# Zero-weight products of a hybrid layer kernel left out from the fifth chunk to the end of the scans

## The chip, the cores and the metric

The kernel runs on one core of a Trainium2 chip. The metric is the device time of one execution in microseconds (us). The core has five engines with a queue each: TensorE (PE, matrix products; its weight loads are listed as PEld), VectorE (DVE), ScalarE (ACT), GpSimd (POOL) and SyncE (SP, which here only issues transfers). Transfers (DMA) are issued from SP and POOL.

## The reference, cut to what matters

The input is x with 8 images of 256 channels and 1024 tokens. Layer 0 is a Mamba block with a forward layer; layer 1 is attention with eight heads and a routed pair of experts for each image.

```python
# layer 0, each image
xz = layernorm(x) @ W_in;  xm, z = split(xz)             # 512 + 512 channels
xm = silu(causal_conv4(xm) + conv_b)
dt, Bm, Cm = split(xm @ W_x);  dt = softplus(dt @ W_dt + b_dt)
for t in tokens:                                          # 16 states a channel
    h = exp(dt[t] * A) * h + (dt[t] * xm[t]) * Bm[t]
    y[t] = sum_s(h * Cm[t])
x = ((y + xm * D) * silu(z)) @ W_out + x
x = gelu(layernorm(x) @ W1 + b1) @ W2 + b2 + x
# layer 1
t = x + attention(ln(x), column bias from edges)          # 8 heads of 32, 1024 x 1024 scores
t = t + layernorm(experts(ln(t)) + ln(t))                 # top 2 of 8, chosen per image
```

## The kernel before

All values are float32 and lie with the channels on the 128 partitions. Tokens are worked in chunks of 512, two to an image, 16 in all (`i` from 0 to 15). In the program a product of float32 operands is one instruction; the profile shows it as two passes (841 zero products in the program, 1682 passes).

**The backbone.** The loop `for now in range(nsteps)` goes over 512 scan steps, 32 to a chunk (`NSTEP`): a step is one of 16 states and one of two halves of the 512 channels. VectorE multiplies the inputs with a row of B (`hb<-xm,bc`), scans over the 512 tokens with the decay from ScalarE (`da_all<-dt,vecs`), and multiplies with the row of C (`hb<-hb,bc`). An accumulating transfer on POOL's queue adds the result up in memory (`dx<-hb`). `bc` is a row of B and of C, broadcast to all partitions by a transfer on SP's queue two states ahead.

**The streams beside it.** All other work is written as generators: `prologue` (norm `mu_a`, `var_a`, projection `xin`, convolution, `dbl`, `v`, softplus), `gate_part` (`z`, silu), `epilogue` (output `mo`, norm `mu_f`, `var_f`, forward layer `fh`, `facc`, norm `mu_t`, `var_t`), attention (`vp`, `qkp`, scores `sc`, exponentials `pt`, sums `num` and `den`, output `wo`, norm `mu_x`, `var_x`) and experts (`he`, `re`, norm `var_y`). In each norm VectorE subtracts a mean that TensorE has just formed (`tn_t<-fo,mu_t` for instance), and works on the variance after it.

**What sets the order.** A planner at build time (`Model`, `Queue`) keeps a clock for each engine with a cost for each kind of instruction, steps its time along VectorE's queue in `advance`, and writes the next piece of a stream when the planned time has come and its buffers and banks are free. Each engine then runs its instructions in the order written. There are two single banks of PSUM (`banks`), two pairs (`pairs`) for scores, and one bank each for `num` and `den`.

**Zero products.** At the end of each planner tick `advance` calls `keep_warm` (L1794). Where TensorE's planned time lies more than 0.2 us behind, it writes one product of 128 x 128 zero weights with 256 columns of a constant. While an attention sum is open it adds zeros to that bank (`num<-mean_c,zero_c` in the profile), else it takes a free single bank and gives it back at once (`warm<-mean_c,zero_c`).

```python
if pe.at > model.t - 0.2:
    return
x = mean_c.to_broadcast([P, CH // 2])
if open_sums:
    pe.matmul(open_sums[-1][:, : CH // 2], zero_w, x, start=False, stop=False)
elif banks.ready():
    ps = banks.now("warm")
    pe.matmul(ps[:, : CH // 2], zero_w, x, start=True, stop=True)
    model.end = pe.at
    banks.put(ps)
```

After the scans `while due: idle(0.25)` (L1947) lets the streams that are left run out: the last image's attention and experts, where the sums of exponentials are on VectorE. A second way to compute (`attention_any` and the block after it) is taken only when a flag on the data asks for it, and does not run here.

Of the kernel before, what the change touches and what calls it, by code (L numbers as in the profile page):

```python
# [28 lines left out]
NSTEP = NHALF * NS  # L29
# [25 lines left out]
def hybrid_kernel(ctx: ExitStack, tc: tile.TileContext, a: dict, out: bass.AP):  # L55
# [21 lines left out]
    model = Model()  # L77
# [40 lines left out]
    pool, pe = Queue(nc.gpsimd, pool_cost), Queue(nc.tensor, pe_cost)  # L118
# [351 lines left out]
            vec.tensor_scalar(w[:, k, cols], w[:, k, cols], V(gain, k), None, ALU.mult)  # L470

    capacity = float(math.ceil(B * L * 1.25 / E))
    set_up = []
    open_sums = []
    ends = {}
# [260 lines left out]
    def load_bc(n):  # L736
        i, s = divmod(n, NS)
        bc = work_pool.tile([P, 2, CH], F32, name=f"bc_{n}", tag="bc", bufs=AHEAD + 1)
        landed = sp.dma_start(
            bc, chunk[i]["bc_d"][s].partition_broadcast(P)  # L740
        )
        bcs[n] = (bc, landed)
# [6 lines left out]
    def decay(g, q):  # L749
        i, s, h = place(g)  # L750
        da = da_all[:, g % 2, q, :]
        n = (2 * h + q) * NS + s


        skip = 1 if q and i % NCH == 0 else 0
        if skip and g % NSTEP < 2:
            act.copy(da[:, :1], zero_c)
        act.activation(
            da[:, skip:], chunk[i]["dt"][h][:, q, skip:], AF.Exp, scale=neg_a[:, n : n + 1]
        )  # L760
        das[g, q] = act.at
        if q and s == NS - 1:
            model.end = act.at
            t4.put(chunk[i]["dt"][h])

    def inputs(g):

        i, s, h = place(g)
        hb = hbs[g] = h4.now(f"hb_{g}")
        bc, landed = bcs[g // NHALF]  # L770
        vec.at = max(vec.at, landed)
        xd = chunk[i]["xd"][h]
        vec.tensor_tensor(hb, xd, bc[:, 0, :].unsqueeze(1).to_broadcast([P, 2, CH]), ALU.mult)
        if s == NS - 1:
            t4.put(xd)

    def scan(g, q):

        i, s, h = place(g)
        c = i % NCH  # L780
        hb = hbs[g]
        d = 2 * h + q
        done = das.pop((g, q))
        vec.at = max(vec.at, done)
        if c == 0:
            if q:
                both = hb.rearrange("p a t -> p (a t)")
                vec.tensor_tensor_scan(
                    both, da_all[:, g % 2].rearrange("p a t -> p (a t)"), both, 0.0,
                    ALU.mult, ALU.add,  # L790
                )
        else:
            vec.tensor_tensor_scan(
                hb[:, q, :], da_all[:, g % 2, q, :], hb[:, q, :], state[:, s, d : d + 1],
                ALU.mult, ALU.add,
            )
        if q and c < NCH - 1:
            pool.tensor_copy(state[:, s, 2 * h : 2 * h + 2], hb[:, :, CH - 1])

    def sums(g):  # L800

        i, s, h = place(g)
        me = chunk[i]
        bc, _ = bcs[g // NHALF] if h < NHALF - 1 else bcs.pop(g // NHALF)
        hb = hbs.pop(g)
        vec.tensor_tensor(hb, hb, bc[:, 1, :].unsqueeze(1).to_broadcast([P, 2, CH]), ALU.mult)
        model.t = vec.at
        me["landed", h] = pool.dma_start(out=me["acc", h], in_=hb, accum_op=ALU.add)
        h4.put(hb, at=me["landed", h])

    def gate_part(i):

        while not set_up:
            yield POLL
        me = chunk[i]
        mem = Owner(t4, 3, 2)
        xn = yield from mem.take(f"xz_{i}")
        yield sp.dma_start(xn, me["xn_d"])
        sz, ps = [], None
        for d in range(ND + 1):  # L820
            if d:
                h, q = divmod(d - 1, 2)
                act.activation(
                    sz[h][:, q, :], ps, AF.Identity, bias=b_in[:, ND + d - 1 : ND + d]
                )
                banks.put(ps)
            if d < ND:
                if d % 2 == 0:
                    sz.append((yield from mem.take(f"sz_{i}_{d // 2}")))
                ps = yield from banks.take(f"z_{i}_{d}")  # L830
                for k in range(KC):
                    pe.matmul(
                        ps, w_in[:, k, DI + d * P : DI + (d + 1) * P], xn[:, k, :],
                        start=(k == 0), stop=(k == KC - 1),
                    )
                yield
        mem.put(xn)
        for t in sz:
            act.activation(t, t, AF.Silu)
        lnexp()  # L840
        mem.end()
        yield
        me["sz"] = sz
# [916 lines left out]
    with tc.tile_pool(name="work", bufs=1) as work_pool:  # L1760
# [30 lines left out]
        def start(stream, key, at=0.0):  # L1791
            due.append([at, URGENT[key[0]], len(done) + len(due), stream, key])

        def keep_warm():  # L1794


            if pe.at > model.t - 0.2:
                return
            x = mean_c.to_broadcast([P, CH // 2])
            if open_sums:  # L1800
# [7 lines that stand above are left out]
        def advance():  # L1808


            while True:
                model.t = min(model.t + TICK, vec.at)
                for d in sorted(due, key=lambda d: d[1:3]):
                    while d in due and d[0] <= model.t + 0.05:
                        if d[1] > 2 and max(pe.at, act.at) > model.t + LAG:
                            break
                        model.end = model.t
                        try:
                            at = next(d[3])
                        except StopIteration:  # L1820
                            due.remove(d)
                            done.add(d[4])
                            break
                        if at == POLL:
                            break
                        d[0] = (model.end if at is None else at) + 0.1
                keep_warm()
                if model.t >= vec.at:
                    break

        def idle(t):

            vec.at += t
            advance()
# [77 lines left out]
        inputs(0)  # L1912
        for now in range(nsteps):
            i, k = divmod(now, NSTEP)
            if i + 1 < B * NCH and k == max(FRONT[i], 1):
                start(prologue(i + 1), ("p", i + 1), model.t)
            if k == GATE[i]:
                start(gate_part(i), ("g", i), model.t)
            n = now // NHALF + AHEAD
            if now % NHALF == 0 and n < B * NCH * NS:  # L1920
                while "bc_d" not in chunk.get(n // NS, {}):
                    idle(0.5)
                load_bc(n)
            if now + 2 < nsteps:
                while "dt" not in chunk.get((now + 2) // NSTEP, {}):
                    idle(0.5)
            for q in range(2):
                scan(now, q)
                advance()
                if now + 2 < nsteps and (q or i % NCH):  # L1930
                    for r in range(0 if i % NCH == 0 else q, q + 1):
                        decay(now + 2, r)
            if now == 0:
                while ("p", 0) not in done:
                    idle(0.25)
                for q in range(2):
                    decay(1, q)
            if now + 1 < nsteps:
                while not h4.free:
                    idle(0.5)  # L1940
                inputs(now + 1)
                advance()
            sums(now)
            if k == NSTEP - 1:
                start(epilogue(i), ("e", i), model.t)
            advance()
        while due:  # L1947
            idle(0.25)

# [264 lines left out]
```

## Time and profile before

| | us |
|---|---|
| median of 3 runs | 3561.6 |
| lowest and highest | 3555.06, 3567.71 |
| profiled execution, its own time | 3553.65 |
| its span, first to last instruction | 3551.9 |
| PE, DVE, ACT, POOL busy in it | 3227.3, 3062.4, 2470.0, 935.7 |
| mean granted TensorE clock | 0.953 |

The span is what views of the trace divide up; the execution's own time lies 1.75 us above it. Busy times of one engine don't overlap, those of several do. A wait is an idle stretch of an engine with what ended it. In the view by windows, each line has the stretch, its length, the busy time of each engine with the number of instructions, the granted clock (1 is full speed), the share of the DMA engines and GB/s. A product's end is modelled, so TensorE's busy share is not its share of peak.

### The profile page before, as it was taken

What the parts mean: (1) busy time and instruction counts of PE and PEld (TensorE: products, weight loads), DVE (VectorE), ACT (ScalarE), POOL (GpSimd) and SP (SyncE); (2) the same over time, 40 slices, a digit from 0 to 9 for tenths busy, and PEclk for the clock granted to TensorE, in tenths of its full rate; (3) what the DMA queues carried; (4) which work ended last, traced back from release to release, by engine and by line L of the source; (5) the groups of instructions that cost most, each with busy time, mean ns of one, the idle gap of its engine ahead of it and who ended that gap; (6) DMA issues with size and microseconds to landing.
All of it is one profiled execution on the core that took longest, in us unless ns stands there. A gap on an engine that the chain in (4) does not pass through costs nothing. (4 is left out here: it accounts for less than half of the span.)

```text
span 3551.9 us, 40220 instructions
## 1 busy us (share of the span) xinstructions
PE 3227.3 (91%) x14535; PEld 1401.8 (39%) x14535; DVE 3062.4 (86%) x3148; ACT 2470.0 (70%) x3563; POOL 935.7 (26%) x1058
## 2 busy tenths in 40 slices
PE   8767879997999899999999999999999999999997
PEld 5544344333433344333443334333433334334344
DVE  6979999899999798999999899989999999943551
ACT  5553737795778776787778867886688776864644
POOL 0232223222332124322322233223432332211010
PEclk9888989999999998999999999999999999999999
DMA  4757978787788778898787987889888878942120
GB/s 121 196 128 159 201 172 195 166 195 180 186 203 202 168 177 190 207 196 196 183 202 182 203 187 188 188 194 210 199 200 186 197 180 192 207 107 70 37 76 15
DMA packets 189504, 607.80 MB, mean 171 GB/s; under 512 B 27056, under 2 KB 38000, under 8 KB 189296
## 3 DMA queue, kind: packets, MB, share of 16 engines
q0 software_dynamic: 103968, 366.54, 53.3%
q1 hardware_dynamic: 85328, 238.60, 20.8%
q8 instruction: 116, 1.90, 0.2%
q14 instruction: 92, 0.75, 0.1%
HBM read 238.58 MB, written 62.39 MB: 85 GB/s over the span
## 5 line engine op out<-in xcount | busy, mean ns | idle before, releaser
L100 ACT ACTIVATE da_all<-dt,vecs 128x512 f32<-128x512 f32 (+1 forms) x1024 | 700.9, 717 | 436.3 <-DVE hb L100 433.1
L95 POOL DMA_DIRECT2D dx<-hb x512 | 444.5, 871 | 1671.2 <-DVE hb L100 1331.3
L100 DVE TENSOR_TENSOR hb<-hb,bc 128x1024 f32<-128x1024 f32 x512 | 625.9, 1222 | 36.9 <-POOL state L100 26.9
L100 DVE TENSOR_TENSOR_SCAN hb<-da_all,state,hb 128x512 f32<-128x512 f32 x512 | 632.2, 1271 | 8.5 <-ACT da_all L100 8.4
L100 DVE TENSOR_TENSOR hb<-xm,bc 128x1024 f32<-128x1024 f32 x512 | 619.2, 1209 | 10.4 <-DMA dx<-hb 10.2
L100 DVE TENSOR_TENSOR_SCAN hb<-da_all,hb 128x1024 f32<-128x1024 f32 x256 | 584.7, 2284 | 2.8 <-ACT da_all L100 2.8
L100 ACT ACTIVATE pt<-sc 128x1024 f32<-128x1024 f32 x512 | 494.1, 1017 | 91.9 <-PE sc L100 81.1
L100 PE MATMUL warm<-mean_c,zero_c 128*128 128x256 f32 x1368 | 411.4, 430 | 35.4 <-ACT dt L100 9.3
L100 PEld LDWEIGHTS warm<-mean_c,zero_c 128*128 128x128 f32 x1368 | 260.0, 206 | 201.4 <-PE warm L100 82.5
L100 PE MATMUL sc<-qk,qk 32*128 32x512 f32 x2048 | 323.5, 644 | 10.9 <-ACT pt L100 10.4
L100 PE MATMUL num<-pt,v 128*32 128x512 f32 x2048 | 280.9, 620 | 43.9 <-DVE ot L100 43.9
L100 POOL COPY state<-hb 128x2 f32<-128x2 f32 x256 | 207.2, 809 | 366.5 <-DVE hb L100 351.3
L100 PE MATMUL den<-pt,ecb 128*32 128x512 f32 x1792 | 243.8, 615 | 0.0
L100 PE MATMUL facc<-fh,w 128*128 128x512 f32 x512 | 231.4, 598 | 3.9 <-DVE xf_x L100 1.8
L100 PE MATMUL fh<-x_f,w 128*128 128x512 f32 x480 | 230.2, 609 | 4.2 <-DVE x_f L100 1.7
L100 PE MATMUL he<-xe,g 128*128 128x512 f32 x448 | 218.5, 612 | 3.6 <-DVE x_f L100 1.8
L100 ACT ACT_TABLE_LOAD x169 | 216.8, 1283 | 3.6 <-PEq L2201 0.7
L100 PE MATMUL re<-he,g 128*128 128x512 f32 x472 | 213.8, 596 | 2.3 <-DVE xn L100 2.2
L100 PEld LDWEIGHTS sc<-qk,qk 32*128 32x128 f32 x2048 | 95.4, 184 | 183.4 <-issue 75.8
L100 PE MATMUL mo<-sz,w_out 128*128 128x512 f32 x256 | 126.4, 639 | 25.8 <-DVE sz L100 24.6
L100 PEld LDWEIGHTS facc<-fh,w 128*128 128x128 f32 x512 | 94.6, 190 | 131.1 <-issue 119.5
L100 PEld LDWEIGHTS fh<-x_f,w 128*128 128x128 f32 x480 | 87.9, 192 | 131.2 <-issue 109.6
(364 smaller groups left out, 4280.4 us busy)
## 6 DMA issues: line engine op xcount, KB each, us to landing
dx<-hb POOLq DMA_DIRECT2D x512, 512.0 KB, 6.5
bc<-bc_d SPq DMA_DIRECT2D x256, 512.0 KB, 4.5
dt<-e POOLq DMA_DIRECT2D x38, 512.0 KB, 8.6
dt<-u POOLq DMA_DIRECT2D x30, 512.0 KB, 9.0
xe<-xf_d SPq DMA_DIRECT2D x28, 512.0 KB, 6.5
xn<-in_x SPq DMA_DIRECT2D x16, 512.0 KB, 7.9
xn_d<-xn SPq DMA_DIRECT2D x16, 512.0 KB, 4.6
xz<-xn_d SPq DMA_DIRECT2D x16, 512.0 KB, 7.2
```

Source lines behind the costliest of these rows:

```text
L95: f(*args, **kw)
L100: return f(*args, **kw)
```

## The change

From the 129th scan step on (`now == 4 * NSTEP`, the first of the fifth chunk) `keep_warm` returns at once, and after the last scan step it works again as before. The list `busy` is the switch. Nothing else is edited; since the planner counts each zero product in TensorE's time and in a bank's, the place of other instructions can move.

```diff
     capacity = float(math.ceil(B * L * 1.25 / E))
+    busy = []
     set_up = []
...
         def keep_warm():
-            if pe.at > model.t - 0.2:
+            if pe.at > model.t - 0.2 or busy:
                 return
             x = mean_c.to_broadcast([P, CH // 2])
...
         for now in range(nsteps):
             i, k = divmod(now, NSTEP)
+            if now == 4 * NSTEP:
+                busy.append(True)
             if i + 1 < B * NCH and k == max(FRONT[i], 1):
                 start(prologue(i + 1), ("p", i + 1), model.t)
...
             advance()
+        busy.clear()
         while due:
             idle(0.25)
```

## The prediction

> **What bounds the kernel now.** I read the page's busy shares and slices first, then three stretches by windows, then what VectorE waits for, then single products in the timeline. One core runs everything, so span and clock need no comparison between cores. On the page, TensorE (PE) seems the fullest engine, VectorE (DVE) the next:
>
> ```profile
> PE 3227.3 (91%) x14535; PEld 1401.8 (39%) x14535; DVE 3062.4 (86%) x3148; ACT 2470.0 (70%) x3563; POOL 935.7 (26%) x1058
> ...
> PEclk9888989999999998999999999999999999999999
> ```
>
> The first 65 us are setup, the scan's chunks run from there to 3134 us, and the fifth chunk's first input product starts at 838 us (counted along VectorE's hb products, 32 to a chunk). So the change acts between 838 and 3134. The windows view gives per stretch the length, then PE, weight loads, DVE, ACT, POOL busy, the granted clock, DMA share and GB/s. The second fence is the same view for the instructions that read the zero column alone:
>
> ```profile
> 838.00:3134.00 2296.00, 2150.03 (x9396) 882.36 (x9392) 2160.68 (x2091) 1751.53 (x2493) 689.18 (x764) 0.97 0.84 193
> 3134.00:3552.00 418.00, 386.87 (x1842) 167.17 (x1838) 152.46 (x298) 212.70 (x268) 32.77 (x35) 0.98 0.19 53
> ```
>
> ```profile
> 838.00:3134.00 2296.00, 199.57 (x628) 113.77 (x628) 2.07 (x11) 0.00 (x0) 0.97 0.84 193
> ```
>
> DVE is busy 2160.7 of 2296 us, 94%. PE is busy 2150.0, but some 200 of that are products with zero weights, so its own work is at most 1950 us, 85%. VectorE sets the pace, and what can change is its 135 us of idle time. Its waits in this stretch (us, times, longest):
>
> ```profile
> DVE hb L100 <- POOL state L100: 19.7, 6, 4.7
> DVE tn_t L100 <- PE mu_t L100: 19.4, 7, 4.4
> DVE xm L100 <- ACT dx L100: 13.0, 1, 13.0
> DVE x_f L100 <- PE mu_f L100: 8.4, 6, 2.4
> DVE xf_x L100 <- PE mu_x L100: 8.2, 4, 3.9
> ```
>
> Those on TensorE, with the smaller rows (var_y 5.6, var_t 4.0, vp 3.1, four rows of 0.4 to 1.0), sum to 51.8 us. The change can take part of them away or add to them.
>
> What makes such a wait is seen in the timeline. The same four passes of a 512-column mean take 1.88 us at full clock (mu_x) and about 3 us or more after an idle stretch (mu_t, mu_f; start, length, instruction, idle before):
>
> ```profile
> 858.39 3.97 PE L100 MATMUL warm<-mean_c,zero_c 128*128 128x256 f32 x16
> 868.28 3.52 PE L100 MATMUL mu_f<-x,mean_c 128*128 128x512 f32 x4 [5.92 <-DMA x<-in_x]
> ```
>
> ```profile
> 2524.07 4.21 PE L100 MATMUL warm<-mean_c,zero_c 128*128 128x256 f32 x8 [0.72 <-DVE z L100]
> 2528.07 3.00 PE L100 MATMUL mu_t<-fo,mean_c 128*128 128x512 f32 x4
> ```
>
> ```profile
> 2376.78 1.88 PE L100 MATMUL mu_x<-xr,mean_c 128*128 128x512 f32 x4
> ```
>
> [...]its clock record for the 2296 us has 23 stretches at 0.5 and nothing else below 1.0, in multiples of 3.4 us, 149.8 us together, which is the windows' 0.97 (1 - 0.5 x 149.8 / 2296).[...]
>
> **The change part by part.**
>
> 1. *Products removed.* The built program drops from 841 zero products to 519: 322 fewer, in 110 runs of about three, 644 passes of 256 columns (the trace shows 628 of them after 838). Nothing else is taken out: DVE 5680, ACT 5598, POOL 1201 and SP 665 instructions stay, every DMA among them. The early chunks and the tail after the scans keep theirs. PE gets up to 199.6 us back, but mostly where it would be idle: gaps between real products sum to 328 us there against 146 us now.
>
> 2. *Clock lost.* I cut the stretch into 672 windows of 3.41 us, in phase with the clock record, and took TensorE's busy share of each from its matmul records. With the zero products 19 windows lie under 0.4, without them 65.[...] So there are 14 stretches more, each as long as now (149.8 / 23 = 6.5 us), 91 us at least; at most 76 windows more, 259 us[...]. What cold time costs DVE: its waits on products that ran in or right after a cold stretch are 4.4, 3.8, 3.7, 3.2, 2.4, 1.9, 1.8, 1.8 and 1.8 us, 24.9 us over 149.8, or 0.17 us per cold us. The rest is hidden, since expert, attention and forward products end in ScalarE evictions and ScalarE is 76% busy. So the loss is 15 to 43 us; I take 22, for some 130 us more of cold time.
>
> 3. *Waits ahead of real products removed.* In front, a run delays a real product by one 256-column product in flight at most (two passes, 3.97 / 8 = 0.50 us), over 110 runs 55 us of PE time, of which DVE sees only what ends in a mean, a variance or a v projection. TensorE's own waits before zero products (on readers of the bank) add 12.6 us in 14 cases. The gain for DVE cannot exceed its waits on PE outside cold stretches, 51.8 - 24.9 = 26.9 us, and may be nothing. I take 8.
>
> 4. *Order moved.* The planner counts zero products in TensorE's time and gives them a bank, so without them other work is placed a little differently: of 5680 DVE instructions 4358 keep their place. Against the scan steps of 6 us, the experts' work lies 4 to 6 steps earlier from chunk 4 on, the attention exponentials 1.1 steps, forward layer and prologue within half a step. At the end nothing is gained: 96 exponentials are left after the last scan before and after, and 54 evictions of he. Loads on SP's queue move by up to 13 places and accumulating transfers on POOL's by up to 23; bc keeps its two steps of lead. A single collision in this stretch costs DVE 4.7 (state) to 13.0 us (dx), so this can go either way: 0, with 10 us on each side.
>
> 5. *Tail.* From 3134 to 3552 DVE is the one that waits and PE is the chain; its zero products remain. Cost 0, within a few us that item 4 covers.[...]
>
> Sum: +22 - 8 + 0 = **+14 us**. The profiled execution took 3553.65 us by its own time (span 3551.9 and 1.75 around it), which makes 3567.7. That execution lies 8 us under the median of the shown runs, 3561.6, and I put the difference on the median: **3576 us**, slower by 0.4%.
>
> **The rivals.** A change over 0.3%, some 10.7 us, is about what a measurement of this kernel can tell from none.
>
> *Zero products were in the way (faster).* One mechanism: real products start earlier where TensorE is behind, between attention and the mean products, and the planner's earlier placing makes it lasting. For it: 110 runs, 12.6 us of bank waits, mu_t held behind eight passes. Against it: of the nine waits listed, only one has a run directly in front; the others have num and den products or nothing. With item 3 at its bound and item 2 at its low end: 15 - 27 = -12, with a lucky order -22: about 3545. It decides once more than half of the 51.8 us goes away.
>
> *TensorE is covered (no change).* DVE instructions stand in an order where a late product is met by work of 1.2 to 2.3 us (one product or scan in flight), and 1.7 us is what four cold passes lose. If this hides nearly every new stretch, the loss falls to 8 and the gain cancels it: 3562.
>
> *The removed products are not the ones that hold the clock.* At 858 sixteen of them ran off in 4 us and the clock still fell. Most gaps over 5 us already end cold. Then item 2 is near zero and the result is rival one or two.
>
> *A long slow stretch.* [...]the clock stays low through whole projections, and attention falls behind: the 43 us end, with the order against it: 3605 or more.
>
> **How the numbers follow.** Slower by over 0.3%: 0.45 (the +14 case and the long slow stretch). No change: 0.28. Faster: 0.27. The range is from the faster rival to the 43 us end with no gain, 3543 to 3606, leaving out one in ten on each side.
>
> **What would show it.** Clock in the fifth to sixteenth chunk: 0.94 rather than 0.97 (about 280 us cold), PE's busy share at 88 to 92%, the four passes of mu_t and mu_f more often at 3 to 3.5 us than at 1.88. DVE's waits on mu, var and vp products up from 51.8 to about 66 us. The last scan at about 3148 us; the tail near 418. I am wrong if the clock stays at 0.96 or above, or if it falls and those waits do not grow, or if the difference lies in waits on POOL, DMA or in the tail: then the order decided.

## The result, and the profile after

The changed kernel takes 3584.86 us (median of 4 runs, 3579.59 to 3590.17) against 3558.78 us for the kernel before (4 runs): ratio 1.007, 95% interval 1.0044 to 1.0095, 26 us slower. The profiled execution took 3590.17 us with a span of 3588.2. It is the slowest of the four, and the profiled one of the kernel before, 3553.65, was faster than that kernel's four, so the two spans differ by 36.3 us. Of these, 4.3 us lie ahead of the fifth chunk, where both kernels have the same order; in the kernels of this document the fifth chunk starts between 838 and 846 us.

The same two lines of its page as were shown of before, TensorE's clock in 40 slices in the second:

```profile
PE 3129.4 (87%) x13891; PEld 1317.7 (37%) x13891; DVE 3063.2 (85%) x3148; ACT 2473.5 (69%) x3563; POOL 941.0 (26%) x1058
...
PEclk9878979997999898999999999999999999999999
```

By windows, from the fifth chunk's first input product (842.7) to the last scan step, and the tail:

```profile
842.70:3167.00 2324.30, 2039.05 (x8744) 789.16 (x8748) 2158.21 (x2084) 1749.25 (x2485) 693.30 (x762) 0.94 0.83 190
3167.00:3588.00 421.00, 391.31 (x1846) 169.01 (x1838) 156.26 (x303) 218.01 (x277) 33.94 (x36) 0.98 0.21 55
```

The stretch grew from 2295.4 to 2324.2 us, the tail from 418 to 421. VectorE's own work is the same to 3 us, so the 29 us are waits. The clock fell from 0.97 to 0.94. TensorE's clock record shows 47 cold stretches (half clock), 300 us together, where it had 23 of 150 us. Had we stopped here, the clock would seem the cause. VectorE's longest waits in this stretch speak against it (waiter, releaser, us, times, longest):

```profile
DVE xm L100 <- DMA dt<-u: 21.2, 6, 6.3
DVE xf_x L100 <- PE mu_x L100: 20.7, 5, 10.5
DVE xm L100 <- ACT dx L100: 17.4, 3, 9.9
DVE hb L100 <- DMA dx<-hb: 15.8, 6, 5.6
DVE e L100 <- ACT u L100: 13.4, 4, 8.5
DVE hb L100 <- POOL state L100: 9.4, 5, 4.7
```

All waits on TensorE sum to 55.1 us, 3 more than before, though single rows moved by more: mu_x from 8.2 to 20.7 us, mu_t from 19.4 to 6.0. What grew most are the waits of the softplus end (xm and e, on ScalarE and the dt transfers): 52.8 us, which were 17.5. Those on the accumulating transfers dx<-hb, the `sz` row with them, went from 4.2 to 18.2 us. At one place three waits follow each other, and the chunk that has them, the eighth, takes 213 us where it took 179. VectorE's timeline at its end:

```profile
1599.13 1.21 DVE L100 TENSOR_TENSOR hb<-hb,bc 128x1024 f32<-128x1024 f32 x1
1608.85 1.23 DVE L100 SCALAR_TENSOR_TENSOR e<-u,e 128x1024 f32<-128x1024 f32 x1 [8.51 <-ACT u L100]
1620.60 1.22 DVE L100 TENSOR_TENSOR xf_x<-xr,mu_x 128x1024 f32<-128x1024 f32 x1 [10.52 <-PE mu_x L100]
1627.05 2.45 DVE L100 TENSOR_TENSOR xm<-xm,dt 128x1024 f32<-128x1024 f32 x2 [5.23 <-ACT dx L100]
```

In 30 us VectorE does five operations, four of them no part of a scan step, and no scan. The three late pieces belong to two streams (softplus of the next chunk; attention's output norm) and stand one after the other in its queue. They wait for 24.3 us together, 13.7 of it at the softplus end. In the kernel before, scan steps stand between such pieces there, and they find their inputs ready:

```profile
1593.85 2.45 DVE L100 TENSOR_TENSOR_SCAN hb<-da_all,state,hb 128x512 f32<-128x512 f32 x2
1596.22 1.20 DVE L100 TENSOR_TENSOR xm<-xm,dt 128x1024 f32<-128x1024 f32 x1
1597.34 1.22 DVE L100 TENSOR_TENSOR hb<-xm,bc 128x1024 f32<-128x1024 f32 x1
...
1600.13 1.22 DVE L100 TENSOR_TENSOR xm<-xm,dt 128x1024 f32<-128x1024 f32 x1
```

### The profile page after: what moved, and what is told of

Its sections match the earlier page's. It is cut to its first block, busy times and chain, and to the rows that moved or that the text cites. A ratio compares the mean times of both kernels' runs of the same rounds, so it can differ in the third digit from the quotient of the medians.

```text
span 3588.2 us, 38949 instructions
## 1 busy us (share of the span) xinstructions
PE 3129.4 (87%) x13891; PEld 1317.7 (37%) x13891; DVE 3063.2 (85%) x3148; ACT 2473.5 (69%) x3563; POOL 941.0 (26%) x1058
## 3 DMA queue, kind: packets, MB, share of 16 engines
q1 hardware_dynamic: 85328, 238.60, 20.6%
## 4 chain that ended last, share of the span: by engine, by line
DVE 37%; PE 31%; issue 11%; ACT 9%; DMA 7%; POOL 4%; DVEq 0%; POOLq 0%; SPq 0%; ACTq 0%
DVE hb L100 27%; PE num L100 4%; DMA dx<-hb 3%; PE sc L100 3%; PE re L100 3%; PE he L100 3%; PE facc L100 2%; DVE xm L100 2%; POOL state L100 2%; PE den L100 2%; PE fh L100 2%; ACT da_all L100 1%; PE warm L100 1%; ACT L100 1%; PE halves L100 1%
## 5 line engine op out<-in xcount | busy, mean ns | idle before, releaser
L100 PE MATMUL sc<-qk,qk 32*128 32x512 f32 x2048 | 352.4, 657 | 28.7 <-ACT pt L100 23.6
L100 PE MATMUL num<-pt,v 128*32 128x512 f32 x2048 | 290.3, 637 | 46.9 <-DVE ot L100 46.9
L100 PE MATMUL warm<-mean_c,zero_c 128*128 128x256 f32 x908 | 265.1, 430 | 17.3 <-ACT dt L100 5.8
L100 PE MATMUL facc<-fh,w 128*128 128x512 f32 x512 | 243.5, 622 | 14.1 <-ACT fh L100 4.1
L100 PE MATMUL re<-he,g 128*128 128x512 f32 x472 | 221.4, 614 | 9.1 <-ACT he L100 6.6
L100 PEld LDWEIGHTS warm<-mean_c,zero_c 128*128 128x128 f32 x908 | 179.6, 210 | 103.3 <-PE warm L100 40.4
L100 PEld LDWEIGHTS sc<-qk,qk 32*128 32x128 f32 x2048 | 104.2, 187 | 227.2 <-ACT pt L100 108.2
L100 PE MATMUL z<-xz,w_in 128*128 128x512 f32 x256 | 130.1, 640 | 10.7 <-ACT sz L100 6.7
```

Source lines behind the costliest of these rows:

```text
L100: return f(*args, **kw)
```

## The experiments

The change does two things at once: it takes products out of TensorE's queue, and it takes their time and bank out of the planner's count, which moves other instructions. The first two experiments hold one and vary the other. A ratio below is estimated from all runs of both kernels and need not be the quotient of the two medians.

**Order of before, products out.** The planner counts the products as before; from the fifth chunk to the end of the scans they are not written (527 are left of 841).

```diff
-                pe.matmul(open_sums[-1][:, : CH // 2], zero_w, x, start=False, stop=False)
+                into = open_sums[-1][:, : CH // 2]
+                model.do(pe, pe.cost("matmul", into, zero_w))
+                if not busy:
+                    pe.engine.matmul(into, zero_w, x, start=False, stop=False)
```

(the same for the product into a free bank)

> 314 zero products are left out between the fifth chunk and the end of the scans, but the planner still counts them in time and banks, so every other instruction of every engine stands exactly where it stands in the kernel before. Clock theory (the loss comes from the products that no longer hold TensorE's clock): the granted clock between 838 us and the last scan falls from 0.97 to about 0.94 and the time rises by 18 to 30 us, as in the changed kernel (ratio 1.005 to 1.008). Order theory (the loss comes from the other placing of experts, transfers and softplus pieces): the clock falls as well, but the time stays within 8 us of before (ratio 0.998 to 1.002). Theory that zero products are in the way: 5 to 15 us faster.

Measured: 3561.26 us against 3559.56, ratio 1.0006 (0.9997 to 1.0015). In the trace the instructions of VectorE, ScalarE and GpSimd stand in exactly the order of the kernel before. The clock is as low as in the changed kernel: 42 cold stretches, 294 us. By windows:

```profile
840.00:3138.00 2298.00, 2035.90 (x8751) 792.49 (x8752) 2159.03 (x2089) 1748.61 (x2493) 693.60 (x763) 0.94 0.85 193
```

Its first waits of VectorE in that stretch stand as in the kernel before:

```profile
DVE tn_t L100 <- PE mu_t L100: 20.4, 7, 4.0
DVE hb L100 <- POOL state L100: 18.9, 8, 4.7
DVE xm L100 <- ACT dx L100: 12.7, 1, 12.7
DVE xf_x L100 <- PE mu_x L100: 9.2, 5, 3.9
```

All its waits on TensorE sum to 51.8 us, the figure of before, with 143 us more at half clock. So the half clock and the absence of the products together cost VectorE next to nothing.

By the total alone, a loss by the clock could be hidden by a gain from the freed queue. Since VectorE's order in this stretch is the same in all kernels with the order of before, their traces can be compared wait by wait. On one side stand this kernel and the one below without any zero product, on the other the kernel before and the one below without products in the tail only; the one with four chunks out counts on either side, by chunk. Nine waits are longer by over 0.2 us in every kernel without products at that place than in every one with them, 8 us together; three are shorter in the same way, 3 us. Both effects are there, then, but small. With two or three executions on each side this gives a size and no exact figure.

**Order of the changed kernel, products back.** Zero products are written by a clock of their own that the planner does not see (849 in all, 330 more than the changed kernel).

```diff
+            if busy:
+                if max(pe.at, shadow[0]) > model.t - 0.2:
+                    return
+                shadow[0] = model.t + pe.cost("matmul", mean_c.to_broadcast([P, CH // 2]), zero_w)
+                ...  # the product itself by pe.engine; the bank goes back with its old time
+                return
```

> The order of the changed kernel for every other instruction, with 330 zero products written where TensorE's planned time lies behind, by a clock of their own that the planner does not see. Clock theory: the granted clock in the stretch is back at 0.96 to 0.97 and the time is within 8 us of the kernel before (ratio 0.998 to 1.002). Order theory: the clock is back, the time stays 18 to 30 us over before (ratio 1.005 to 1.008).

Measured: 3580.72 us, ratio 1.0058 (1.0042 to 1.0074), 21 us slower than before, though the clock is back (0.97, 27 cold stretches, 120 us). VectorE, ScalarE and GpSimd have exactly the order of the changed kernel in the trace.

```profile
844.00:3163.00 2319.00, 2165.80 (x9412) 875.91 (x9412) 2158.97 (x2085) 1747.38 (x2486) 691.24 (x763) 0.97 0.84 191
```

The pile-up at the end of the eighth chunk is the same to within 1.2 us:

```profile
1602.86 1.23 DVE L100 SCALAR_TENSOR_TENSOR e<-u,e 128x1024 f32<-128x1024 f32 x1 [7.39 <-ACT u L100]
1614.61 1.22 DVE L100 TENSOR_TENSOR xf_x<-xr,mu_x 128x1024 f32<-128x1024 f32 x1 [10.52 <-PE mu_x L100]
1621.06 2.45 DVE L100 TENSOR_TENSOR xm<-xm,dt 128x1024 f32<-128x1024 f32 x2 [5.22 <-ACT dx L100]
```

The two experiments settle which of the two carries the loss: the order (21 of 26 us; the rest is within the intervals), while the absence of the products carries next to none. They don't say what in the order does it.

**Products out in four chunks only**, the fifth to the eighth, in the order of before (`busy.clear()` at the ninth).

> As the kernel with the order kept, but the zero products are left out in the fifth to eighth chunk alone (145 of the 314). Clock theory: if the loss goes with the number of products left out, 46% of that kernel's loss, some 8 to 14 us (ratio 1.002 to 1.004), clock near 0.92 in these four chunks and 0.97 after them. Order theory: no change within 5 us.

Measured: 3558.53 us, ratio 0.9999 (0.9988 to 1.0009). The clock theory's 8 to 14 us are not there.

**Products out everywhere**, in the order of before (`busy = [True]` from the start, none of 841 written).

> The order of the kernel before for every other instruction, and no zero product written anywhere, while the planner counts all 841. Order theory (products cost and bring nothing where VectorE sets the pace, and the time follows from the order alone): within 8 us of before (ratio 0.998 to 1.002), though the clock falls to about 0.90. Clock theory for the early chunks and setup, where TensorE waits most: 10 to 40 us slower, most of it before 838 us.

Measured: 3564.98 us against 3561.58, ratio 1.0011 (1.0003 to 1.0019): all zero products together are worth some 4 us. The clock by windows falls to 0.75 in setup and the first four chunks, where it was 0.90:

```profile
0.00:838.00 838.00, 501.40 (x2461) 208.93 (x2461) 745.92 (x758) 503.32 (x798) 214.08 (x259) 0.75 0.74 169
838.00:3134.00 2296.00, 2027.42 (x8746) 788.76 (x8746) 2156.75 (x2085) 1749.59 (x2492) 694.58 (x762) 0.94 0.84 193
3134.00:3557.00 423.00, 357.03 (x1649) 137.64 (x1648) 159.69 (x307) 215.13 (x274) 34.62 (x37) 0.92 0.21 56
```

**Products out in the tail only**, in the order of before (`busy.append(True)` ahead of the last `while due:`).

> The kernel before in its own order, with zero products everywhere but after the last scan: the 117 there are counted by the planner and not written. In this tail TensorE is busy 387 of 418 us and in the chain that ends last, and 120 zero products more had cost about 20 us, most of it in the tail. If products in front of real ones are what counts there: 5 to 20 us faster than before (ratio 0.994 to 0.999). If the clock counts there: 0.98 falls to some 0.9 and the time rises by 5 to 20 us. Neither: no change.

Measured: 3555.31 us against 3560.89, ratio 0.9992 (0.9983 to 1.0001). Neither expected effect shows; as a faster version it is not established. The tail takes 417 us, as before (418), at a lower clock (0.945 over the whole execution, 0.953 before; the kernel without any zero product shows 0.92 in its tail, the kernel before 0.98), so a small loss and a small gain may cancel here; no run separates them.

**More products.** Six ahead of the first sums of an attention group, where a bank is free (120 in all), unseen by the planner:

```diff
+                if held[2] == 0:
+                    for _ in range(6):
+                        ...  # if banks.ready(): one zero product by pe.engine
                 pe.at = max(pe.at, free if held[2] == 0 else 0.0)
```

> The kernel before in its own order, with 120 zero products more: six in front of the first sums of an attention unit group, where TensorE waits for VectorE's ot (43.9 us in 18 waits) and where several cold stretches follow; the planner does not count them. Clock theory: fewer cold stretches after those waits, clock up by about 0.01, and 3 to 12 us faster than before. Order theory: no change within 5 us, or up to 8 us slower where the six delay the sums.

Measured: 3581.35 us, ratio 1.0058 (1.0041 to 1.0075), slower, and by more than any of the expected cases. The stretch up to the last scan took 2302.4 us (before 2295.4), the tail 435.9 (before 418.2). In the tail VectorE's sums (dsum) wait longer for ScalarE's exponentials; in the kernel before that wait was 47.4 us in 20 times, and the first line here was the same:

```profile
DVE r L100 <- ACT r L100: 59.6, 6, 31.0
DVE dsum L100 <- ACT pt L100: 59.1, 22, 19.8
```

Sixty of the added passes ran in the tail, about 13 us at the 218 ns from one to the next that zero passes have at full clock in the kernel before (median of 1191 such pairs). Put there, directly in front of sums, products are paid for. The kernel's own zero products in the tail are not, by the run before this one.

**Other orders.** I then asked what in the order is bad. In the program one can see, for each chunk's prologue, where its two input products `xm<-xm,dt` stand on VectorE. At the last place that the planner has, it waits for them itself. Both stand there in four of the prologues 5 to 15 before, in seven after the change. Five kernels have other orders. The first starts prologues earlier in the changed kernel, the next two count another planned cost for zero products in the stretch, and two begin the change later. (The kernels with another planned cost write 826 and 946 zero products.)

```diff
-    FRONT = (8, 1, 6, 2, 6, 9, 6, 3, 12, 2, 13, 3, 7, 5, 7)
+    FRONT = (8, 1, 6, 2, 3, 6, 3, 1, 9, 1, 10, 1, 4, 2, 4)
```

> The changed kernel, with the prologue of each chunk from the sixth on started three scan steps earlier (FRONT[i] - 3, not below 1, for i from 4). The place theory: the loss comes from prologues that the planner finishes only at the last place it has, where VectorE's input products xm<-xm,dt stand against ScalarE and the accumulating transfers of dt. Of the prologues 5 to 15, four have both of these products at that last place in the kernel before, seven in the changed one, five here; with 26 us for three more, 8 to 9 us each, this gives some 3567 us (ratio to before 1.001 to 1.004). Lottery theory (the hand-set tables fit the order before, and any other order loses alike): 3575 to 3590. Clock theory, already weak: as the changed kernel, 3585.

Measured: 3623.31 us against 3560.89, ratio 1.0187 (1.0168 to 1.0205).

```diff
+            cost = 0.58 if busy else pe.cost("matmul", x, zero_w)    # 0.38 in the other
...
-                pe.matmul(open_sums[-1][:, : CH // 2], zero_w, x, start=False, stop=False)
+                pe.engine.matmul(open_sums[-1][:, : CH // 2], zero_w, x, start=False, stop=False)
+                model.do(pe, cost)
```

> The kernel before with its zero products, but the planner counts 0.58 us for one instead of 0.46 from the fifth chunk to the end of the scans. Seven prologues stand at their last place, as in the changed kernel. Place theory: 3578 to 3590 (ratio 1.005 to 1.009), with the waits of xm on dx and dt and of e on u over 30 us together. Clock theory: within 8 us of before. Lottery theory: 3575 to 3590 as well.

Measured: 3611.21 us, ratio 1.015 (1.0129 to 1.0171).

> As the one before, with 0.38 us in place of 0.46. Five prologues stand at their last place. Place theory: some 3567 us (ratio 1.001 to 1.004). Lottery theory: 3575 to 3590. Clock theory: within 8 us of before.

Measured: 3602.2 us, ratio 1.0121 (1.0104 to 1.0138).

```diff
-            if now == 4 * NSTEP:
+            if now == 8 * NSTEP:    # 12 * NSTEP in the other
```

> The change with its start at the ninth chunk instead of the fifth, so that the order stays that of before up to 1610 us. If the loss of the changed kernel lies in the placing around the end of its eighth chunk (213 us for that chunk against 179): within 10 us of before. If any other order loses (lottery): 15 to 40 us slower, all of it after 1610 us. Clock theory: 8 chunks of 12, some 17 us, spread evenly.

Measured: 3602.49 us against 3561.58, ratio 1.0115 (1.0099 to 1.013).

> The change with its start at the thirteenth chunk, 2388 us. Few instructions move. Order theory: a difference only after 2388 us, where it follows from single new waits of VectorE: between 5 us faster and 20 us slower. Clock theory: 4 chunks of 12, some 9 us slower.

Measured: 3571.76 us, ratio 1.0031 (1.0019 to 1.0043).

The place theory falls as an account of the loss: orders with five late prologues lose 62 and 41 us, more than the 26 of the changed order with seven, and the kernel that keeps the order up to the ninth chunk, and so has no pile-up at the end of the eighth, loses 41. Late prologues do cost something: with a planned cost of 0.58 seven are late, and the softplus end waits for 65.2 us (xm on dx and dt, e on u). The lottery theory (any order other than that of before loses alike) missed the size: the first three lose 41 to 62 us where it said 14 to 29. What the orders lose, each loses elsewhere. With the start at the ninth chunk it is in norms and softplus after 1610:

```profile
DVE fo L100 <- ACT fo L100: 20.4, 3, 11.5
DVE e L100 <- ACT u L100: 17.6, 5, 8.4
DVE tn_t L100 <- PE mu_t L100: 10.5, 4, 5.9
```

With a planned cost of 0.38 the softplus end is nearly as before (20.6 us), and waits on TensorE are up, 70.5 us in all where they were 51.8 (v from 3.1 to 14.2, var_t from 4.0 to 7.2), as is fo on ScalarE (2.3 before):

```profile
DVE hb L100 <- POOL state L100: 23.9, 7, 6.3
DVE tn_t L100 <- PE mu_t L100: 18.3, 8, 5.9
DVE fo L100 <- ACT fo L100: 15.6, 5, 7.5
DVE v L100 <- PE vp L100: 14.2, 4, 4.6
```

With the start at the thirteenth chunk the last four chunks take 743 us, no more than before (746). Its 10 us lie in the tail, 427 us, where VectorE's wait for mu_x alone takes 13.8 us (5.0 before). So a change of order that begins in the stretch can show in the tail alone.

The table sets the kernels side by side, from the profiled executions (the stretch from the fifth chunk to the last scan, the tail, and VectorE's waits in the stretch with a releaser in the profile, us):

| order of | kernel | clock, whole | stretch | tail | waits |
|---|---|---|---|---|---|
| before | before | 0.953 | 2295 | 418 | 116 |
| before | products out in the stretch | 0.929 | 2298 | 419 | 120 |
| before | out in four chunks | 0.944 | 2297 | 418 | 118 |
| before | out everywhere | 0.892 | 2299 | 416 | 120 |
| before | out in the tail | 0.945 | 2291 | 417 | 113 |
| before | 120 more | 0.956 | 2302 | 436 | 123 |
| changed | changed | 0.930 | 2324 | 421 | 144 |
| changed | products back | 0.953 | 2318 | 420 | 139 |
| own | prologues earlier | 0.930 | 2347 | 433 | 166 |
| own | planned cost 0.58 | 0.947 | 2341 | 421 | 161 |
| own | planned cost 0.38 | 0.949 | 2330 | 429 | 152 |
| own | from the ninth chunk | 0.934 | 2333 | 431 | 156 |
| own | from the thirteenth | 0.943 | 2304 | 427 | 123 |

The stretch follows the order, 2291 to 2302 us in all six kernels with the order of before, whatever the clock. No other order comes as low, though the one that starts at the thirteenth chunk, 2304, is not apart from them; in most of the others the tail is longer as well.

## Why the prediction was right, and which step failed

The forecast of slower by 14 us had the right sign, and its range, 3543 to 3606, held the time; the reason given for it was wrong. That the sum came out on the right side was luck: a cost of the clock that is hardly there stood in for a cost of the order that was left at 0.

- *Products removed, clock lost.* The count was right: 130 us more of cold time was taken, 150 came (143 with the order kept), with the clock at 0.94 as said. The 130, between 91 and 259, was an estimate of mine, by a rule for the clock's falls and returns that no trace here shows. **The price was the step that failed**: 0.17 us of VectorE's waits per cold us, 22 us in all. The kernel with the order kept has the cold time and a loss of 1.7 us, not separable from none; compared wait by wait, some 8 us of longer waits stand against 143 us of cold time, about 0.06. The price was drawn from nine waits of one execution, 24.9 us. The same nine sum to 18.8 us in the kernel with products out in the tail only, whose stretch has the same products, order and clock, and to 20.5 us with the order kept and the low clock. So part of the 24.9 was the chance of one execution, and most of the rest is there at either clock. That the waits lay in cold stretches showed no cause.
- *Waits ahead of real products.* The 8 us of gain are not there as a gain in time (0.9999 and 1.0006); wait by wait, some 3 us are.
- *Order moved.* **This is the second step that failed.** The term was put at 0 with 10 us on each side, and it is +21 us by itself, nearly the whole result. I had priced a single collision at 4.7 to 13 us. The one at the end of the eighth chunk takes 24.3 us (8.51 + 10.52 + 5.23), because three late pieces follow each other in a queue without a scan step between them to hide behind.
- *Tail.* Right: 421 us, no change to speak of.
- *What would show it.* I had written that I am wrong if the clock falls and the mean, variance and v waits don't grow. They went from 51.8 to 55.1 us with all small rows, the `logits` row among them, not to 66. The other sign, a difference in waits on transfers, came true: those rows went from 6.5 to 39.4 us (dt<-u and dx<-hb, `sz` included). Those two signs did their work before any experiment.
- *Rivals.* That products were in the way fell. (Its time was summed loosely: 3561.6 less 22 is 3540, not 3545.) "TensorE is covered" was right as to the clock, and would have been the result had the order stayed. Its 1.7 us for four cold passes was about right: in the fifth to sixteenth chunk of the kernel before, four passes of a mean took 1.88 to 1.98 us at full clock, and 3.75 and 3.78 us in the two cases wholly at half clock. That the removed products don't hold the clock fell with the 150 us more of cold time; all three gaps of TensorE over 5 us in these chunks ended at half clock before, and all eleven after. A long slow stretch did not form: the longest cold one is 17.1 us before and after.

Open is what makes the order of before better than each of the six other orders that ran. The start tables (`FRONT`, `GATE`) are constants that fit one order, so that any shift would meet them badly; this is argued from the losses of 10 to 62 us, and not shown, since no tables were fitted to a new order. For the pile-up itself I saw one link only: in the changed program the second half's softplus step `e` stands five scan steps later than before, at 254.5 in place of 249.5, next to `xf_x`, which came forward from 256.5. Whether the prologue lacked free buffers there was not tested.

## What to carry to other kernels

Where a planner at build time orders all queues, an edit of one cheap instruction is two edits: what the engine runs, and where everything else is put. Let the planner count what you leave out, and you measure the first alone; write it unseen by the planner, and you measure the second. Here it took two kernels to show that the obvious mechanism, a clock seen to fall (0.97 to 0.94), was not the one that cost the time.

A wait that coincides with a slow clock is not yet a wait caused by it; compare the same wait at both clocks before giving it a price.

## What the runs showed of the hardware

In this kernel a mean TensorE clock of 0.75 in a stretch went without a loss that counts. With no zero product at all the mean granted clock was 0.892, and 0.75 in the first 838 us, where it was 0.90 before, for a loss of 0.1% in all; the fifth chunk then starts at 842 us, between the 838 and 846 of the other kernels. The windows fit this: TensorE is busy for 501 of the first 838 us even at the lower clock, while VectorE is busy for 746.

The clock did not fall after idle time alone. The clock record of the kernel before has 47 falls to half, and 3.41 us is its shortest length between two changes. In the 3.41 us ahead of a fall TensorE's busy share (from the matmul records) was under 10% in nine cases, 29% in the median, over half in eleven and 91% in one. Of the 888 pieces of the same length after which the clock stayed at full, 95% were over 72%, and the lowest was at 43%.
